# A four-layer graph network on one core: products of the identity in TensorE's waits

## The chip, the cores and the metric

The kernel runs on one core of a Trainium2 chip. The metric is the time on the device, in microseconds (us). A core has five engines that work side by side and wait for each other by semaphores: TensorE (PE; PEld is its loading of weights), VectorE (DVE), ScalarE (ACT), GpSimd (POOL), and SyncE (SP), which here issues the loads of the large matrix. TensorE's clock can be granted in full or in part, and the profile records which.

## What is computed

x is 4096 x 64, adj is 4096 x 4096 and sparse, with values of 0.05 to 1 where it is not zero. Four layers follow each other, each with `h = relu(layernorm(x))` and `x = x + layer(h, adj)`:

```
layer 0:  relu((adj @ h) @ W.T + b)
layer 1:  att = adj * sigmoid((2 + 2 * qm @ k.T) / att_scale + att_bias)
          support = att @ lorentz(h);   support / sqrt(|inner(support)|)
layer 2:  agg_i = sum_j adj_ij / deg_i * logmap(h_i, h_j);   expmap0(agg @ W + b)
layer 3:  mask = adj != 0;  w = mask * 0.5 ** (rank from the row's end, 100 neighbours at most)
          w @ (h @ W) + b
```

Layer 1's q and k are two more linear maps of the layer's own h, each scaled row by row. Layer 2 needs a square, a clamp, two logarithms and two exponentials for every pair (i, j). Layer 3 needs a running count of neighbours along each row.

## The kernel before, in words

adj is read transposed, in pieces of 128 x 1024 f32 (512 KB, "groups"): a group holds two chunks of 128 source rows for one block of 512 target rows. There are 8 blocks (`ib`) of 16 groups (`g`). Each layer reads the groups that it needs from memory again, through `feed` (SP's queue) into ten buffers, six of them kept for all layers. A buffer is free again when its last reader on each engine is done.

- Layer 0: `l0_sums` multiplies each group with the rows of h (`HA`), two matmuls of 64 columns side by side, into one bank `acc`; DVE adds the groups up for the degrees (`dg`). `before0` makes h from x, block by block, and group g needs the rows of block g/2. At the end of a block `after0` updates x, and `before1` makes q, k and the rows for layer 1.
- Layer 1: `l1_atts` (PE, into `mm`), `l1_sigmoids` (ACT), `l1_weights` (DVE, times adj), `l1_sums` (PE, into `acc`), in pairs of groups; at a block's end `after1` and `before2`.
- Layer 2: distances on PE (`l2_dists`), square on ACT, clamp on POOL, then ACT and DVE in turn, transposes on PE (`l2_turns`, into the banks `tr`), and two kinds of sums. It uses that a pair's distance is symmetric: blocks get shorter from one to the next.
- Layer 3: masks on DVE, counts and ranks in bf16 matmuls, powers of two on ACT (`wt`), sums in bf16.

Two banks `tr` serve everything that is small: transposes, small products and the degrees. `bank` takes one from the list `spare`, and `emptied` puts it back as soon as the reader of its content has been written into the program, which can be before that reader has run.

The order on each engine is fixed while the program is built. Each stage is a generator that yields the engine that its next step uses and the time from which it may run. `in_turn` always takes the step that can start first, by a clock kept in the source (`Pace`): `pace.free[engine]` is when an engine gets free, `pace.now` when the chosen step starts. `Pace.issue` moves an engine's clock on by the instruction's modelled cost, from the time when the engine and the tiles with known ready times are free. Tiles named in `KEPT` (x, HA, qT and others) have no such time, so PE's clock may lag behind the step's own start. Everything is issued through `InOrder.__getattr__` (line 129 in the profile), so the profile's groups are told apart by their tiles, not by lines. Each engine runs its instructions in that order.

Of the kernel before, what the change touches and what calls it, by code (L numbers as in the profile page):

```python
# [18 lines left out]
P = 128  # L19
# [6 lines left out]
G = 2  # L26
NG = NC // G
LEFT = (3, 7, 11, 15)
EARLY = 12
BEHIND = NG - CB // G  # L30
LATE = BEHIND - CB // G
# [105 lines left out]
def kernel(ctx: ExitStack, tc: tile.TileContext, a: dict, out: bass.AP):  # L137
# [4 lines left out]
    pace = Pace()  # L142
    PE, DVE, ACT, POOL = (
        InOrder(tc, e, pace, name)
        for e, name in (
            (nc.tensor, "PE"), (nc.vector, "DVE"), (nc.scalar, "ACT"), (nc.gpsimd, "POOL"),
        )
    )
# [11 lines left out]
    x = keep.tile([P, NC, D], F32, name="x")  # L160
# [4 lines left out]
    ident = const.tile([P, P], F32, name="ident")  # L165
# [168 lines left out]
    spare = [0, 1]  # L334

    def bank():
        k = spare.pop(0)
        t = ps_tr.tile([P, W], F32, tag=f"tr{k}", name="tr", bufs=1)
        in_use.append((t, k))
        return t  # L340

    def emptied(t):
        k = [k for k in in_use if k[0] is t][0]
        in_use.remove(k)
        spare.append(k[1])
# [334 lines left out]
    tail = []  # L680
# [7 lines left out]
    def advance(entry):  # L688
        pace.latest = 0.0
        old = entry.pop("bank", None)  # L690
        before = len(in_use)
        if not entry["evicts"]:
            if entry["slot"] is None:
                entry["slot"] = 1 - tail[0]["slot"] if entry is not tail[0] else (
                    1 - tail[1]["slot"] if len(tail) > 1 and tail[1]["slot"] is not None else 0
                )
            slot["now"] = entry["slot"]
        entry["evicts"] = False
        on = next(entry["gen"], tail)
        if on is tail:  # L700
            tail.remove(entry)
        else:
            entry["on"], entry["at"], entry["need"] = on, pace.latest, None
            if isinstance(on, tuple):
                entry["on"], entry["need"] = on
        if len(in_use) > before:
            entry["bank"] = in_use[-1][0]
        if old is not None:
            emptied(old)
# [4 lines left out]
    def in_turn(threads):  # L714

        waiting = [[gen, next(gen, None)] for gen in threads]
        waiting = [t for t in waiting if t[1]]
        while waiting or tail:  # L720
            best = None
            for k, entry in enumerate(tail):
                if k < 2 or entry["evicts"]:
                    need = entry["need"]() if entry["need"] else 0.0
                    if need is None or (entry["on"] == TURN and not spare):
                        continue
                    start = max(entry["at"], pace.free[entry["on"]], need)
                    if "tables" in opened and "weighed" not in work[FIRST]:
                        start += 2 * EPS
                    if best is None or start < best[0]:  # L730
                        best = start, entry
            for thread in waiting:
                on, need = thread[1]
                t = need()
                if t is not None and (best is None or max(t, pace.free[on]) < best[0] - EPS):
                    best = max(t, pace.free[on]), thread
            pace.now, what = best
            if what in tail:
                advance(what)
                continue  # L740
            pace.latest = 0.0
            what[1] = next(what[0], None)
            if what[1] is None:
                waiting.remove(what)


    st = {
# [4 lines left out]
    opened = {}  # L752
# [67 lines left out]
    def group(layer, ib, g):  # L820
        degree = (g in LEFT and 0 < ib < NB - 1) == (layer == 1)
        return {"layer": layer, "ib": ib, "g": g, "degree": degree, "left": 1 + degree, "at": 0.0}
# [6 lines left out]
    l1 += [group(1, ib, g) for ib in range(2, NB) for g in range(NG)]  # L829
    order = l0[: len(l0) - EARLY] + [d for pair in zip(l0[len(l0) - EARLY :], l1) for d in pair]  # L830
    order += l1[EARLY:]
    done = {}
# [571 lines left out]
    def l3_sum():  # L1404
# [25 lines left out]
    last = work[L3_AT:]  # L1430
    order23 = work[:L3_AT] + [d for pair in zip(last, l3) for d in pair] + l3[len(last) :]
    in_turn([
        feed(order, "early"), feed(order23, "second"), second_tables(), second_part(), third_part(), l2_loads2(),
        l0_sums(), l1_sums(), l1_weights(), l1_sigmoids(), l1_atts(),
# [59 lines left out]
```

## Time and profile before

| | |
|---|---|
| time, median of 3 runs | 1186.83 us (1185.45 to 1261.08) |
| profiled execution | 1186.61 us, its span 1184.6 us |
| mean granted TensorE clock | 0.976 |
| busy: PE, DVE, ACT, POOL | 1078.5, 929.3, 783.1, 324.3 us |
| matmul records on PE | 5367 |
| read from memory | 269.68 MB, 229 GB/s over the span |
| adj groups loaded | 512 |

The page's rows of digits show the span in 40 slices, PEclk the granted clock in tenths. In a row of the timeline the first number is the start in us from the span's start, the second the time until the last of the merged instructions ended, then engine, operation, out<-in tiles, shapes and count; square brackets hold the engine's idle time ahead of it and what ended that. Ends of matmuls are modelled, and a 512-column f32 matmul takes two records. By the timeline, layer 0 lasts until about 220 us (mixed with the start of layer 1), layer 1 until 486, layer 2 until about 957, and layer 3 until the end.

### The profile page before, as it was taken

The page shows a single profiled execution, that of the slowest core. Times are in us where ns is not written, and L with a number is a line of the kernel's source. Part 1 is how long each engine was busy: PE and PEld are TensorE (multiplying, and loading weights), DVE is VectorE, ACT ScalarE, POOL GpSimd, SP SyncE. Part 2 cuts the span into 40 slices and gives each one's busy share as a digit, 9 for nine tenths or more (in the row PEclk, how much of TensorE's full clock was granted, in tenths as well). Part 3 has the DMA queues.
Part 4 walks back from the last instruction along what each step waited for, and adds up shares of the span by engine and source line. Part 5 has one row for each costly group of instructions (what it writes and reads, how often), then busy time and mean ns, then how long its engine had stood idle before and what let it go on. Part 6 is the DMA issues. An engine that isn't in the chain of part 4 may idle for free.

```text
span 1184.6 us, 15638 instructions
## 1 busy us (share of the span) xinstructions
PE 1078.5 (91%) x5367; PEld 449.7 (38%) x5392; DVE 929.3 (78%) x1523; ACT 783.1 (66%) x1250; POOL 324.3 (27%) x172
## 2 busy tenths in 40 slices
PE   3899999999999999889989989999889789999997
PEld 1234444333333333244444444444344333333332
DVE  6888888869988988688888888898989985555550
ACT  1055456777767766789988778787876655555554
POOL 2222321102000010344454464464654420000000
PEclk9898999999999999899999999999998999999999
DMA  7899999865777765535434534444364389888830
GB/s 275 330 405 350 401 378 348 303 216 199 245 249 235 249 232 192 195 107 196 162 128 172 175 121 166 160 150 163 113 206 151 124 343 367 321 314 312 303 112 9
DMA packets 77191, 271.76 MB, mean 229 GB/s; under 512 B 10040, under 2 KB 11064, under 8 KB 77112
## 3 DMA queue, kind: packets, MB, share of 16 engines
q1 hardware_dynamic: 75456, 270.57, 63.7%
q8 instruction: 42, 0.69, 0.2%
q10 hardware_dynamic: 1656, 0.20, 0.1%
q14 instruction: 37, 0.30, 0.1%
HBM read 269.68 MB, written 1.05 MB: 229 GB/s over the span
## 4 chain that ended last, share of the span: by engine, by line
PE 49%; DVE 18%; ACT 11%; issue 10%; POOL 8%; DMA 3%; SPq 0%; ACTq 0%; POOLq 0%; DVEq 0%
PE acc L129 23%; PE mm L129 17%; PE tr L129 8%; DVE dg L129 5%; POOL v L129 4%; ACT wt L129 3%; DVE w L129 3%; ACT v L129 2%; DMA adj<-in_adjT_dram 2%; ACT t L129 2%; DVE t L129 2%; POOL lo_s L129 1%; DVE sig L129 1%; ACT sig L129 1%; POOL ln_r L129 1%
## 5 line engine op out<-in xcount | busy, mean ns | idle before, releaser
L129 PE MATMUL acc<-w,HA 128*65 128x256 f32 (+1 forms) x736 | 256.3, 485 | 13.0 <-DVE others L129 7.1
L129 POOL TENSOR_SCALAR v<-v 128x1024 f32<-128x1024 f32 x72 | 204.8, 2845 | 211.5 <-ACT v L129 205.4
L129 ACT ACTIVATE wt<-mm 128x1024 uint16<-128x1024 f32 x124 | 120.3, 1021 | 94.1 <-PE mm L129 94.1
L129 ACT ACTIVATE sig<-mm,att_b,att_a 128x1024 f32<-128x1024 f32 x128 | 148.3, 1202 | 40.9 <-PE mm L129 39.9
L129 DVE TENSOR_TENSOR sig<-sig,adj 128x1024 f32<-128x1024 f32 x128 | 152.5, 1221 | 25.2 <-ACT sig L129 25.0
L129 PE MATMUL acc<-adj,HA 128*64 128x512 f32 x512 | 128.4, 639 | 24.3 <-DVE HA L129 24.1
L129 DVE TENSOR_TENSOR dg<-dg,adj 128x1024 f32<-128x1024 f32 x114 | 139.2, 1221 | 2.2 <-DMA adj<-in_adjT_dram 0.6
L129 PEld LDWEIGHTS acc<-w,HA 128*65 128x65 f32 x736 | 98.1, 143 | 104.7 <-issue 56.6
L129 PE MATMUL mm<-qT,kT 64*128 64x512 f32 x512 | 129.5, 619 | 3.3 <-ACT sig L129 3.3
L129 PE MATMUL acc<-sig,HL 128*64 128x512 f32 x512 | 123.3, 604 | 1.6 <-DVE sig L129 1.5
L129 DVE SCALAR_TENSOR_TENSOR t<-mm,t 128x1024 f32<-128x1024 f32 x72 | 83.6, 1161 | 44.4 <-ACT t L129 43.9
L129 PE MATMUL acc<-wt,S 128*64 128x512 bf16 (+1 forms) x479 | 97.7, 387 | 3.5 <-issue 2.4
L129 PE MATMUL mm<-RT,LT 64*128 64x512 f32 (+1 forms) x288 | 79.7, 631 | 15.9 <-DVE t L129 15.2
L129 ACT ACTIVATE t<-t 128x1024 f32<-128x1024 f32 x72 | 72.6, 1008 | 31.9 <-DVE t L129 31.3
L129 ACT ACTIVATE v<-mm 128x1024 f32<-128x1024 f32 x72 | 69.8, 970 | 30.7 <-PE mm L129 30.6
L129 POOL TENSOR_TENSOR ln_r<-ln_v,minus_half 128x4 f32<-128x4 f32 x32 | 49.3, 1542 | 148.7 <-DVE ln_v L129 148.7
L129 DVE TENSOR_TENSOR w<-t,adj 128x1024 f32<-128x1024 f32 x72 | 84.0, 1167 | 1.5
L129 DVE SCALAR_TENSOR_TENSOR t<-t,v 128x1024 f32<-128x1024 f32 x72 | 83.7, 1163 | 1.8 <-ACT t L129 0.9
L129 ACT ACTIVATE v<-v,minus 128x1024 f32<-128x1024 f32 x72 | 78.4, 1089 | 7.8 <-POOL v L129 7.7
L129 DVE TENSOR_TENSOR w<-tr,adj 128x512 f32<-128x512 f32 x120 | 77.5, 681 | 1.1 <-PE tr L129 1.1
L129 PE MATMUL tr<-ident,t 128*128 128x128 f32 x480 | 66.1, 280 | 11.9 <-DVE t L129 8.2
L129 DVE TENSOR_SCALAR RT<-adj 128x1024 bf16<-128x1024 f32 x74 | 50.4, 698 | 33.3 <-PE mm L129 33.0
(208 smaller groups left out, 1395.6 us busy)
## 6 DMA issues: line engine op xcount, KB each, us to landing
adj<-in_adjT_dram SPq DMA_DIRECT2D x512, 512.0 KB, 4.8
x<-in_x_dram SPq DMA_DIRECT2D x4, 256.0 KB, 3.7
out_dram<-h SPq DMA_DIRECT2D x8, 128.0 KB, 2.8
b<-in_b_dram ACTq DMA_DIRECT2D x2, 32.0 KB
W<-in_W_dram ACTq DMA_DIRECT2D x3, 16.0 KB, 4.4
W0T<-in_W0T_dram ACTq DMA_DIRECT2D x2, 16.0 KB, 3.4
W1T<-in_W1T_dram ACTq DMA_DIRECT2D x1, 16.0 KB, 3.4
W1T<-in_b_dram ACTq DMA_DIRECT2D x1, 0.2 KB
```

The lines of the kernel that those rows point to most:

```text
L129: done = self.tc.keep_in_program_order(getattr(self.engine, op)(*args, **kw))
```

## The change

Each time that `in_turn` has chosen a step on PE, a new function `keep_warm` looks at how long, by the source's clock, PE will have waited for it. If that is 0.6 us or more, a bank `tr` is spare and layer 3 has not been opened, it takes a bank and issues f32 products of the 128 x 128 identity with itself (at the very first place, with 128 columns of x), as many as fit in the wait less 0.2 us at 0.28 us each, 24 at most. Nothing reads them. The bank is given back at once.

```
+WAIT = 0.6
...
             pace.now, what = best
+            on = what["on"] if what in tail else what[1][0]
+            if on == "PE":
+                keep_warm(pace.now - pace.free["PE"])
             if what in tail:
...
+    def keep_warm(wait):
+        if wait < WAIT or not spare or "third" in opened:
+            return
+        t = bank()
+        cold = not pace.shape
+        for _ in range(min(int((wait - 0.2) / 0.28), 24)):
+            PE.matmul(
+                t[:, 0:P], ident, x[:, 0:2, :].rearrange("p c d -> p (c d)") if cold else ident,
+                start=True, stop=True,
+            )
+        emptied(t)
```

The products are issued through the same layer as everything else, so they move PE's clock in the source, and with it the choice of later steps. They use PE and a bank; no other engine and no queue gets an instruction more.

## The prediction

> **What bounds the kernel now.** I read the page first (busy shares, the clock row, the chain), then cut the span where the granted clock changes, then the timeline of TensorE around each place where the change puts instructions.
>
> ```profile
> PE 1078.5 (91%) x5367; PEld 449.7 (38%) x5392; DVE 929.3 (78%) x1523; ACT 783.1 (66%) x1250; POOL 324.3 (27%) x172
> PEclk9898999999999999899999999999998999999999
> PE 49%; DVE 18%; ACT 11%; issue 10%; POOL 8%; DMA 3%; SPq 0%; ACTq 0%; POOLq 0%; DVEq 0%
> ```
>
> TensorE is busy 91% of the span and holds half of the chain that ended last. Its clock is near full nearly everywhere: the mean is 0.976. Even if every cold moment sat on the path, little could be won. Cutting at the clock's steps shows where they are:
>
> ```profile
> 31.20:38.00 6.80, 5.90 (x14) 1.67 (x16) 6.20 (x16) 0.93 (x3) 3.17 (x3) 0.51 0.86 301
> 92.60:99.50 6.90, 6.90 (x23) 3.32 (x24) 6.73 (x12) 4.45 (x22) 1.91 (x1) 0.51 0.90 338
> 99.50:488.60 389.10, 376.45 (x1798) 145.76 (x1794) 325.27 (x594) 258.86 (x583) 58.25 (x34) 1.00 0.77 272
> 488.60:498.80 10.20, 8.44 (x20) 2.63 (x20) 8.67 (x16) 7.22 (x11) 5.62 (x3) 0.51 0.57 213
> 611.50:614.90 3.40, 2.93 (x10) 1.44 (x7) 3.33 (x6) 3.37 (x5) 1.97 (x2) 0.51 0.00 0
> 946.00:952.80 6.80, 6.58 (x21) 3.31 (x21) 5.90 (x12) 3.43 (x6) 2.37 (x1) 0.51 0.34 99
> ```
>
> The columns after the bounds are the length, the busy time of PE, PEld, DVE, ACT and POOL, then the granted clock and the DMA share. There are eleven such half-clock stretches, each about 3.4 us or a multiple of it (41.4, 505.7, 700.2, 775.3, 840.2 and 891.4 are the others). Together they last 58 us, so 29 us is the ceiling of the gain. (16.7 to 21.0 is cold too: there is no record of it, but loads of weights come 0.62 us apart, and 0.29 later.) Layer 1 (99.5 to 488.6) has none. Layers differ in their limit: layer 0 from 60 to 210 us has a DMA share of 0.9 to 1.0; layer 1 has PE busy 233.6 of 240 us; in layer 2 PE, DVE, ACT and POOL take turns in the chain.
>
> **What the Trainium skill says.** "TensorE: Matmul & The Clock Gate", section "What's actually happening": the default clock is half, a free-running window of 3413 ns is watched, and a busy one gives the full clock. The trace agrees: 0.5 and 1.0 only, and stretches that are multiples of 3.41 us. The same page, "HAM oscillation — how this bites in real kernels", gives the rule that only idle gaps over about 3.4 us let the clock fall. The trace disagrees: before the stretch at 611.5 the longest idle time of PE is 1.72 us. A window less than about half busy is enough (1.7 us of 3.4 there; 1.4 of 3.4 before 31.2). Its section "What overlaps and what doesn't" has matmuls in strict order: so a filler that stands before a needed matmul and isn't done delays it. The prices below come from the trace.
>
> **The price of one product.** The added product is f32, 128 columns out, as the one with WqkT (65 rows instead of 128):
>
> ```profile
> 92.71 2.02 PE L129 MATMUL tr<-WqkT,columns 65*128 65x128 f32 x8
> 94.66 1.98 PE L129 MATMUL acc<-adj,HA 128*64 128x512 f32 x4
> ...
> 203.01 1.16 PE L129 MATMUL tr<-WqkT,columns 65*128 65x128 f32 x8
> 204.10 0.65 PE L129 MATMUL acc<-adj,HA 128*64 128x512 f32 x2
> ```
>
> Each f32 product is two records, so these are four products: 1.09 us to the next start at full clock, 0.27 each (0.224 start to start inside the batch), and 1.95/4 = 0.49 at half clock (0.43 start to start). I take 0.224 and 0.43 for long batches.
>
> **The change, part by part.** The built programs differ by 199 added products: 24 ahead of the first sum of layer 0, 61 among its first 14 groups, 39 in layer 1, 25 where layer 2 starts, 41 in its later blocks, 9 ahead of layer 3. That is 45 us of PE work at 0.224. Nothing is removed. Because products advance the source's clock for PE, the order in layers 0 and 1 also shifts a little (the first after0 comes three groups earlier, transposes trade places with sums); from the end of layer 1 on the orders agree. No load moves on SP's queue.
>
> *Start of layer 0.*
>
> ```profile
> 16.70 7.53 PE L129 MATMUL acc<-adj,HA 128*64 128x512 f32 x24 [16.70 <-DVE HA L129]
> 24.52 1.94 PE L129 MATMUL acc<-adj,HA 128*64 128x512 f32 x8 [0.30 <-DVE HA L129]
> ...
> 42.16 10.18 PE L129 MATMUL acc<-adj,HA 128*64 128x512 f32 x40 [3.42 <-DVE HA L129]
> ```
>
> The first 24 wait for the first quarter of x (4.4 us) and end by 4.4 + 24 x 0.43 = 14.7 even cold: free, ahead of 16.7. Then comes the odd piece: 24 products stand between the first group and the second, which is ready at the same time. From 16.7 to 42 PE has 14 groups (0.43 us warm) and 48 products: 6 + 10.8 = 16.8 us. With the clock cold until 21.0, as now, add 2 to 4 us: done by about 37; 13 products more, 2.9 us, about 40. The last HA rows come at 41.7 in any case, because of DVE's constants. Group 14 is then no later. Behind the products wait the releases of buffers: SP issues loads 10, 11, 12 now at 18.7, 21.2, 22.7; load 11 would go at about 25 and 12 at 28. Loads 14 to 21 go from 28.6 to 36.9 anyway, DVE's additions need load 11 first at 35.6. So 0, with bounds -1 and +10.
>
> *Layer 1.* No cold stretch, so nothing to win, and PE is the limit. Where products go, the real waits are shorter than those of the source's clock:
>
> ```profile
> 249.22 2.23 PE L129 MATMUL mm<-qT,kT 64*128 64x512 f32 x8 [0.68 <-ACT sig L129]
> ...
> 357.77 2.23 PE L129 MATMUL mm<-qT,kT 64*128 64x512 f32 x8 [0.21 <-ACT sig L129]
> ...
> 390.61 1.99 PE L129 MATMUL mm<-qT,kT 64*128 64x512 f32 x8
> ```
>
> At 249.2 nine products (2.0) face 0.68 idle and 0.16 of drain: +1.2. At 357.8 three (0.67) face 0.37: +0.3, and again at 427.6. At 390.6 and 460.3 three face no wait: +0.6 each. Four single ones: +0.2 each. Four at 285.8 are taken up by the 1.54 us wait at 288.4, five pairs just fit into waits near 0.5. Sum +3.8; the waits at 252, 259 and 284 give back about 1.5: +2.2, bounds +0.5 and +5 (order included).
>
> *Start of layer 2.* The chain runs through cold PE work:
>
> ```profile
> 492.78 1.12 PE L129 MATMUL tr<-ident,t 128*128 128x128 f32 x4
> ...
> 494.09 3.65 PE L129 MATMUL acc<-w,HA 128*65 128x512 f32 x4 [0.19 <-PE tr L129]
> ```
>
> The same four records take 1.93 at 499.67. Nine products fill 487.3 to 489.4, within an idle 2.77, so the window before 488.6 is 2.7 of 3.4 busy: the clock should hold. The sum saves 1.7, the distances after it 0.6; six products and one more then stand in the way for about 0.3: -2.0, bounds -3.5 and +1.
>
> *Block ends of layer 2.* At 605.4 PE waits 1.31 and gets four products (0.9), free. The cold comes later, from the idle 1.72 before 610.32. There no bank is free and nothing is added. The three at 612.3 come in the cold: 1.3 us against 0.68 free, +0.6 on PE, but the chain runs over POOL's clamp at 614.79, not PE. -0.5 in all, bounds -3 and +2.
>
> *Start of layer 3.* 946 to 952.8 is cold and dense on PE (6.58 of 6.80), and in the chain. Five products fall into the idle 1.67 before 944.65: the window before 946 rises from 1.1 to 2.2 of 3.4 busy, over half. Warm, 6.8 us of work take 3.4; DVE is close behind, so -2.5, bounds -3.4 and 0.
>
> Sum: 0 + 2.2 - 2.0 - 0.5 - 2.5 = -2.8. The profiled execution took 1186.61 us with a span of 1184.6; less 2.8 is 1183.8. The median, 1186.83, is 0.2 above that execution: 1184.
>
> **The rivals.**
> 1. *Products in the way at the start: slower.* If the clock is cold through 16.7 to 42, 14 groups at 0.9 and 48 products at 0.49 take 36 us: group 14 starts about 53 plus 13 x 0.49, late by up to 17; loads wait on the releases, and the DMA-bound layer 0 can't make it up except for about 6 us in which SP waits for DVE (36.9 to 43.3). It decides from about 42 us on. 1184 + 11 = 1195. For: the second batch has no wait behind it. Against: dense work warmed the clock within 4.3 us at 16.7 to 21.0.
> 2. *The clock does not hold.* The windows run free, and most products stand where PE was warm. Then only layer 1 counts: 1187 + 2.5, about 1189. For: the block ends' gap stays empty.
> 3. *All of it helps.* The windows at the block ends and at 92.6 turn warm as well, and each half of 3.4 us counts: 1184 - 10 = 1174. Against: chain on POOL, layer 0 bound by DMA.
>
> **How the numbers follow.** Forecast (1178 to 1188) 0.5, rival 1 0.2 (1190 to 1200), rival 2 0.2 (1187 to 1191), rival 3 0.1 (1170 to 1178). The range leaves out half of rival 3 and the upper part of rival 1: 1176 to 1197. Over 2% is 23.7 us, about what a measurement here can tell from no change; 29 us is the ceiling of a gain, 17 the worst start: faster 0.02, same 0.93, slower 0.05.
>
> **What would show it.** Right: clock 1.0 from 488 to 499 and from 946 to 953; group 14 at 42 us and layer 0's end where they were; layer 1 some 2 us longer between its first distances and the table load; half clock still near the block ends. Wrong: the first sums spread past 42 us with DMA share below 0.9 after it (rival 1), or half clock at layer 2's and 3's start (rival 2). An order that lets ACT run dry in layer 1 would be outside of all of these.

## The result, and the profile after

The changed kernel takes 1184.57 us (median of 12 runs, 1181.51 to 1187.42). The kernel before took 1185.35 us beside it, so the ratio is 0.9992 with a 95% interval of 0.998 to 1.0004: 0.9 us less, between 2.4 less and 0.5 more. One run of before, 1261.08 us, was in a slow state and is left out of the ratio. All differences in us below that are not read from a trace are worked out from such ratios, and can differ by a few tenths from the differences of the medians. The profiled execution took 1184.66 us with a span of 1182.9.

The time is the one forecast, within 0.6 us. The median of before was 1.5 us lower in this comparison than in the first runs, so the gain is 0.9 us and not the 2.8 of the sum. The sum was also put together from wrong parts, as the stages show: that the time fits so closely is luck.

The page of the kernel after, with the lines that answer to those shown of before:

```profile
span 1182.9 us, 16429 instructions
PE 1114.5 (94%) x5765; PEld 494.6 (42%) x5790; DVE 929.3 (79%) x1523; ACT 783.8 (66%) x1250; POOL 321.1 (27%) x172
PEclk9999999999999999999999999999999889999999
PE 54%; DVE 17%; ACT 11%; issue 9%; POOL 6%; DMA 1%; SPq 0%; ACTq 0%; POOLq 0%; DVEq 0%
```

TensorE has 398 records more, two for each of the 199 products. It is busy 36 us longer, and its share of the chain rose from 49 to 54%, in a span that is 1.7 us shorter. The half clock fell from 58 to 24 us in these two profiles (the last, slack microseconds of the program left out). If every one of these moments had held up the end, about 17 us would have been won.

The stretches of the kernel after, cut where the prediction looked (columns as before: length; busy time of PE, PEld, DVE, ACT and POOL; granted clock; DMA share; GB/s):

```profile
21.00:42.00 21.00, 21.00 (x121) 11.06 (x120) 19.51 (x52) 1.76 (x5) 7.40 (x17) 1.00 0.65 244
60.00:203.80 143.80, 140.47 (x747) 62.19 (x743) 128.11 (x201) 81.34 (x306) 32.30 (x20) 1.00 0.99 390
203.80:482.30 278.50, 276.53 (x1302) 107.39 (x1300) 227.37 (x444) 195.81 (x356) 30.59 (x18) 1.00 0.69 229
482.30:499.00 16.70, 14.88 (x90) 8.79 (x88) 13.22 (x21) 14.49 (x20) 10.31 (x6) 1.00 0.53 192
938.50:941.90 3.40, 3.40 (x13) 2.24 (x12) 2.85 (x11) 0.68 (x2) 0.00 (x0) 0.50 0.02 5
942.80:953.00 10.20, 9.91 (x53) 4.61 (x52) 9.10 (x21) 5.74 (x9) 2.37 (x1) 1.00 0.44 157
955.50:958.90 3.40, 3.11 (x13) 0.54 (x12) 3.14 (x8) 1.76 (x4) 1.51 (x2) 0.50 0.90 325
```

The same cuts of layers 0 and 1 in the kernel before:

```profile
60.00:211.50 151.50, 143.86 (x750) 63.77 (x746) 130.34 (x202) 81.50 (x305) 38.00 (x21) 0.98 0.97 377
211.50:485.60 274.10, 267.62 (x1224) 97.71 (x1222) 227.54 (x447) 194.87 (x358) 29.41 (x19) 1.00 0.69 232
```

Three things are to be seen. Layer 0, after its start, is 7.7 us shorter at a DMA share of 0.99 instead of 0.97, where the sum had put nothing; 1.8 us of that is a first HA row (the rows of h that all of layer 0 waits for) that ended later in this profile of before. Layer 1 is 4.4 us longer, and TensorE is busy 8.9 us more in it. Around the start of layer 3 the clock is full from 942.8 to 953, as forecast, but half before it and again after it.

The table puts the stages of all the traces side by side, in us. "Layer 0" runs from the end of the first HA row to the end of the last sum (the row's own end differs by up to 1.9 us between executions, whatever the kernel); "layer 1" from there to its last sum; "start" from the third to the seventh distance of layer 2 (a distance is one group's `l2_dists`); "rest" from there to the end. "Cold" counts the half-clock stretches of 3.4 us in layer 1. "Order" is that of the work in layers 0 and 1; the kernels with old order or no products stem from the experiments below.

| kernel | layer 0 | layer 1 | cold | start | rest |
|---|---|---|---|---|---|
| before | 194.9 | 274.0 | 0 | 27.0 | 667.5 |
| before, again | 194.1 | 277.3 | 2 | 25.4 | 666.2 |
| after | 189.0 | 278.5 | 0 | 24.8 | 671.2 |
| after, again | 189.0 | 280.1 | 1 | 26.0 | 671.6 |
| new order, no products | 189.5 | 280.3 | 2 | 25.8 | 666.8 |
| new order, none in layer 0 | 190.2 | 278.5 | 0 | 25.6 | 669.2 |
| new order, none in layer 1 | 189.0 | 278.7 | 1 | 24.8 | 671.2 |
| old order, all products | 195.8 | 279.6 | 0 | 24.8 | 671.9 |
| new order in layer 0 alone | 189.3 | 276.7 | 1 | 26.7 | 667.3 |
| new order in layer 1 alone | 193.3 | 281.9 | 2 | 25.4 | 667.4 |
| old order, later blocks' products | 194.5 | 277.3 | 2 | 25.4 | 669.8 |
| old order, layer 3's products | 194.9 | 277.3 | 2 | 27.7 | 671.0 |
| old order, products at layer 2's start | 192.8 | 274.0 | 0 | 24.8 | 666.0 |
| new order in layer 0, products at layer 2's start | 190.7 | 276.7 | 1 | 24.8 | 666.2 |

A half-clock stretch in layer 1 costs 1.65 us: 277.3 less 274.0 is two of them, 280.1 less 278.5 one, and the other kernels with layer 1's old order and no products there fit (274.0 with none, 277.3 twice with two). The kernel before has none in one execution and two in another. That its first trace has no cold stretch there is therefore chance. A trace is one execution: those of layer 3's products (1192.34 us) and of layer 2's start (1179.11) are the slowest and the fastest of 22 of their kernels, so only stages are compared here, and gains are taken from the ratios.

### The profile page after: what moved, and what is told of

Same layout as the page of the kernel before. It is cut to its first block, busy times and chain, and to the rows that moved or that the text cites. A ratio compares the mean times of both kernels' runs of the same rounds, so it can differ in the third digit from the quotient of the medians.

```text
span 1182.9 us, 16429 instructions
## 1 busy us (share of the span) xinstructions
PE 1114.5 (94%) x5765; PEld 494.6 (42%) x5790; DVE 929.3 (79%) x1523; ACT 783.8 (66%) x1250; POOL 321.1 (27%) x172
## 4 chain that ended last, share of the span: by engine, by line
PE 54%; DVE 17%; ACT 11%; issue 9%; POOL 6%; DMA 1%; SPq 0%; ACTq 0%; POOLq 0%; DVEq 0%
PE acc L130 26%; PE mm L130 18%; PE tr L130 10%; DVE dg L130 4%; ACT wt L130 3%; POOL v L130 3%; ACT v L130 2%; DVE w L130 2%; ACT t L130 2%; DVE t L130 2%; DVE sig L130 1%; DMA adj<-in_adjT_dram 1%; POOL r_nn L130 1%; ACT sig L130 1%; POOL lo_s L130 1%
## 5 line engine op out<-in xcount | busy, mean ns | idle before, releaser
L130 PE MATMUL acc<-w,HA 128*65 128x256 f32 (+1 forms) x736 | 250.7, 477 | 10.3 <-DVE w L130 5.2
L130 ACT ACTIVATE sig<-mm,att_b,att_a 128x1024 f32<-128x1024 f32 x128 | 148.9, 1201 | 53.1 <-PE mm L130 52.5
L130 PE MATMUL acc<-adj,HA 128*64 128x512 f32 x512 | 120.8, 601 | 2.1 <-DVE HA L130 2.1
L130 ACT ACTIVATE v<-v 128x1024 f32<-128x1024 f32 x72 | 72.8, 1012 | 2.3
```

What stands on the lines that cost most here:

```text
L130: done = self.tc.keep_in_program_order(getattr(self.engine, op)(*args, **kw))
```

## The experiments

The theory after the result: products advance the source's clock for TensorE, which lags behind the steps otherwise, so the change is two changes: another order of the work in layers 0 and 1, and products. The rival is the prediction's account, in which only the products count.

**The order alone.** The source's clock is moved as by the products, and the bank is rotated, but no product is issued.

```
+        moving = x[:, 0:2, :].rearrange("p c d -> p (c d)") if cold else ident
+        n = min(int((wait - 0.2) / 0.28), 24)
+        if not issued(pace.now):
+            spare.append(spare.pop(0))
+            for _ in range(n):
+                pace.issue("PE", "matmul", (Unwritten, ident, moving), dict(start=True, stop=True))
+            return
```

`issued` returns False here; `Unwritten` stands for the bank in the source's clock.

> The order of the change without its 199 products: the source's clock is moved as if they were issued. Theory P (the products keep the clock up, and the order is of no account): layer 0's last sum ends near 211 us as before, half-clock stretches as before (about 58 us), total 1185. Theory O (the order of layers 0 and 1 is what moves layer 0): its last sum ends near 204 as with the change, layer 1 takes some 4 us less than with the change since nothing stands in its way, and the total is 1179 to 1183.

1183.09 us beside 1186.32, ratio 0.9975 [0.9966, 0.9983], so 3.0 us faster, and layer 0 is 189.5 against 194.9 and 194.1. The order alone gains 3.0 us where the whole change gained 0.9. Layer 1 does not come out 4 us shorter than with the change, as theory O had it: it takes 280.3 us, of which two cold stretches are 3.3.

**The products alone.** The order of before, and the 199 products ahead of the same steps (two batches of layer 1 are one pair of groups later), issued past the source's clock.

```
+PRODUCTS = {
+    0: 24, 2: 24, 4: 9, 8: 3, 12: 3, 16: 3, 20: 3, 24: 3, 28: 13, 582: 9,
...
+    2204: 4, 2220: 3, 2300: 1, 2356: 4, 2372: 3, 2517: 3, 2521: 1, 2525: 5,
+}
...
+            if on == "PE" and pace.steps in PRODUCTS and spare:
+                products(PRODUCTS.pop(pace.steps), not pace.steps)
```

> The order of the kernel before, with the 199 products ahead of the same steps as in the change. Theory P: layer 0's last sum ends near 204 us, half-clock time about 28 us, layer 2's start 2 us shorter, layer 1 4 to 5 us longer, total 1183 to 1186. Theory O: layer 0 ends at 211, layer 1 is 4 to 5 us longer, layer 2's start 2 us shorter, total 1187 to 1190.

1193.1 us, ratio 1.0053 [1.0033, 1.0073]: 6.3 us slower. That is more than theory O had (1187 to 1190). Layer 1 takes 279.6 us against 274.0, with no cold stretch in either; the rest takes 671.9 against 667.5 and 666.2. Products without their order lose, about as much in the rest as in layer 1.

**Without layer 1's products, and without layer 0's.** The order is that of the change; the products of one layer move the source's clock only.

```
 def issued(now):
-    return False
+    return not 60.0 < now < 495.0
```

and

```
-    return False
+    return now > 60.0
```

> The order of the change, with the 39 products of layer 1 left out. If these products are what makes layer 1 longer: from the end of layer 0 to the last sum of layer 1 takes 274 us as before instead of 278.5, total 4 us below the change, about 1180.5. If layer 1's new order is what costs: no difference to the change, 1184.5.

> The order of the change, with the 85 products of layer 0's first 41 us left out. Theory P: layer 0's last sum ends near 211 us, half-clock stretches there as before, total 1191. Theory O: its last sum ends near 204 or earlier, total 1184 or less.

Without layer 1's products: 1186.22 us, 1.0005 [0.9991, 1.002]. Without layer 0's: 1185.09, 0.999 [0.9976, 1.0004]. Against the change (0.9992) that is 1.5 us slower without layer 1's products and 0.2 faster without layer 0's, each known to about 2 us, so neither differs measurably from the change. The first run's total is nearer to the second of its forecasts (1184.5) than to the first (1180.5), and its layer 1 takes 278.7 us and not 274: most of what makes it longer is the order. What layer 1's products do there is seen in TensorE's waits for the results of `l1_sigmoids`, ahead of the next `l1_atts`. The line gives the wait in all, the number of times and the longest, for the kernel before:

```profile
PE mm L129 <- ACT sig L129: 3.3, 8, 0.7
```

for the new order with no product:

```profile
PE mm L141 <- ACT sig L141: 7.9, 13, 2.3
```

and for the change:

```profile
PE mm L130 <- ACT sig L130: 0.7, 3, 0.3
```

The new order makes `l1_atts` wait for ScalarE's sigmoids, 4.6 us more, and the products then lie in that wait. ScalarE in its turn waits longer for TensorE, 52.5 us instead of 37.6; before and new order:

```profile
ACT sig L129 <- PE mm L129: 37.6, 36, 3.2
```

```profile
ACT sig L141 <- PE mm L141: 52.5, 42, 3.9
```

The products are not free for all that: with the cold stretches taken off, layer 1 takes 277.0 us in the new order without its products (278.7 less one, 280.3 less two) and 278.5 with them. The time of the whole kernel does not show this 1.5 us.

**The order of one layer.** No products; the source's clock is moved only up to 60 us of its own time (the new order in layer 0, the old one nearly throughout layer 1), or only from 60 to 495 us (the old order in layer 0, the new one in layer 1).

```
-        if wait < WAIT or not spare or "third" in opened:
+        if wait < WAIT or not spare or pace.now > 60.0:
```

and

```
+        if wait < WAIT or not spare or not 60.0 < pace.now < 495.0:
```

> No products; the source's clock is moved as if they were issued, but only in the first 60 us. That gives layer 0 the order that the change has, and layer 1 the order of before from its 20th group or so on. Theory: the new order of layer 0 gains and the new order of layer 1 loses. Then layer 0's last sum ends 3 to 7 us earlier than before, layer 1 takes 274 us from there (280 with the whole order of the change), total 1179 to 1182. If layer 0's gain in the trace was luck of the clock's windows: total 1185 to 1186.5. If the two orders are coupled, a layer 0 that ends earlier only makes layer 1 wait: layer 1 takes 278 to 280 us again.

> The order that the products bring to layer 1, without any product, and with the order of before in layer 0: the source's clock is moved only between 60 and 495 us of its own time. Theory from the traces: that order makes TensorE wait for ScalarE's sigmoids (7.9 us instead of 3.3) and costs about 3 us in layer 1: 1189, with the time from the end of layer 0 to the last sum of layer 1 near 277 us against 274. Rival from the medians (the new order throughout 1183.1, in layer 0 alone 1182.6): it costs half a microsecond, and the rest of those 3 us was half-clock stretches in those executions: 1186.7.

In layer 0 alone: 1182.62 us beside 1186.21, 0.9967 [0.9956, 0.9978], 3.9 us faster. In layer 1 alone: 1189.15 beside 1186.08, 1.0022 [1.0013, 1.0031], 2.6 us slower, and its 281.9 us less two cold stretches (3.3) are 278.6 against 274.0. One order gains, the other loses. Two stages missed their forecasts: this layer 1 was to take 277 us, and that of the first kernel 274, where it took 276.7 with one cold stretch, so about 1 us of layer 0's gain is lost again in layer 1. The waits in this last kernel are those of the new order:

```profile
PE mm L141 <- ACT sig L141: 8.8, 15, 2.3
```

**The products of one place.** The order of before, with the 25 products where layer 2 starts, the 41 in its later blocks, or the nine ahead of layer 3.

```
+PRODUCTS = {1158: 9, 1164: 6, 1168: 1, 1176: 2, 1178: 4, 1184: 3}
```

```
+PRODUCTS = {1286: 2, 1508: 4, 1524: 3, 1724: 1, 1780: 4, 1796: 3, 1956: 1, 2012: 4,
+            2028: 3, 2148: 1, 2204: 4, 2220: 3, 2300: 1, 2356: 4, 2372: 3}
```

```
+PRODUCTS = {2517: 3, 2521: 1, 2525: 5}
```

> The kernel before with the 25 products at layer 2's start alone. Theory: they keep the clock at full from 488 to 499 us, so layer 2's fifth distance comes 2 to 3 us earlier counted from layer 1's last sum, and the total falls by 1.5 to 2.5 us. If DVE's work on the first blocks takes the time anyway: no change of the total (within 0.7 us).

> The kernel before, with only the 41 products that the change adds in the later blocks of layer 2, ahead of the same steps; the order of everything else is that of before. The prediction priced them at -0.5 us (bounds -3 and +2): 1185.7 beside 1186.2 for before. Theory that they stand in the way there (the traces with them take about 4 us more from the seventh distance of layer 2 to the end): 1188 to 1190, and the time from that distance to the last sum of layer 2 near 440 us instead of 436.6. Rival: that was the luck of where the clock's windows fell in those executions: 1186 +- 1, with that stage between 436 and 440 and fewer or more half-clock stretches to match.

> The kernel before, with only the nine products that the change adds ahead of layer 3. The prediction priced them at -2.5 us (bounds -3.4 and 0), because the clock would hold through the dense 6.8 us: 1183.7 beside 1186.2 for before, with full clock where layer 3 starts. Theory that the window before it is still under half busy, or falls elsewhere: 1186 +- 1 and half clock there. Theory that they stand in the way: above 1187.

Start of layer 2: 1184.63 us, 0.9987 [0.9974, 0.9999], 1.5 us faster, and 24.8 us in that stage, against 27.0 and 25.4. Later blocks: 1185.91, 0.9999 [0.9986, 1.0012], no difference that can be measured. Ahead of layer 3: 1187.1, 1.0014 [1.0004, 1.0024], 1.7 us slower where the prediction had 2.5 faster. The theory that the later blocks' products stand in the way (1188 to 1190) failed, that of layer 3's (above 1187) held.

The traces say why the last two don't gain. In the later blocks all distances, counted from the seventh, stand as in the kernel before to within 0.01 us up to the first place where products come. TensorE's timeline there, before (the second profile of it):

```profile
537.38 1.88 PE L129 MATMUL acc<-w,HA 128*65 128x512 f32 x4
539.19 1.13 PE L129 MATMUL mm<-RT,LT 64*128 64x512 f32 x4
```

and with the later blocks' products:

```profile
537.00 1.88 PE L132 MATMUL acc<-w,HA 128*65 128x512 f32 x4
539.32 0.71 PE L760 MATMUL tr<-ident 128*128 128x128 f32 x4 [0.44 <-DVE w L132]
539.96 1.13 PE L132 MATMUL mm<-RT,LT 64*128 64x512 f32 x4
```

The distances had no wait. Two products are put ahead of them, into a bank `tr` that DVE is still reading: TensorE waits 0.44 us for DVE, then multiplies for 0.64, and the next distance comes 1.14 us late (2.96 us after the sums' start instead of 1.81). From there to the last block the difference stays between 0.8 and 1.3 us, apart from single distances that are late for one block: the three and four products of each later block end cost nothing, and bring 0.2 us in all. The last block adds 1.5 us, in a half-clock stretch at 930.6. Five of the six traces with these products have a stretch at that place, about 12 us ahead of the end of the wait shown next, and none of the eight without; why is not shown. The ratio of this kernel shows no loss; its profiled execution took 2.6 us more than its median.

Ahead of layer 3, before (second profile):

```profile
940.36 0.43 PE L129 MATMUL tr<-ident,e 65*128 65x65 f32 x4 [1.59 <-DVE w L129]
940.86 3.38 PE L129 MATMUL acc<-w,HA 128*65 128x256 f32 x8
944.48 0.66 PE L129 MATMUL tr<-ident,l 128*64 128x128 f32 x4 [0.23 <-DVE l L129]
...
958.73 2.46 PE L129 MATMUL acc<-wt,S 128*64 128x512 bf16 x7
```

and with the nine products:

```profile
943.41 0.91 PE L759 MATMUL tr<-ident 128*128 128x128 f32 x6 [1.59 <-DVE w L131]
944.37 0.70 PE L131 MATMUL tr<-ident,e 65*128 65x65 f32 x4
944.86 0.74 PE L759 MATMUL tr<-ident 128*128 128x128 f32 x2
945.39 3.07 PE L131 MATMUL acc<-w,HA 128*65 128x256 f32 x8
948.30 1.28 PE L759 MATMUL tr<-ident 128*128 128x128 f32 x10
949.63 0.63 PE L131 MATMUL tr<-ident,l 128*64 128x128 f32 x4
...
963.79 3.78 PE L131 MATMUL acc<-wt,S 128*64 128x512 bf16 x16
```

The 1.59 us of waiting are still there, and the products come after them: they wait for the same DVE instruction as the work that they were to shorten the wait for. Counted from the end of that wait, the first products cost 0.96 us, the next 0.52, the sums are 0.71 shorter at a partly better clock, and the last five cost 1.33: together 2.1, so `tr<-ident,l` starts 6.22 us after the wait instead of 4.12. That is no luck of one execution: it is 4.1 in all eight traces without these products, 6.0 to 6.3 in five of the six with them, and 4.7 in the sixth, whose clock is full there.

The first sum of layer 3 comes 20.38 us after the wait. In this second profile of before it is 18.37, and in the first, with its half clock from 946.1 to 952.8, 20.13. The other six traces without these products fall into the same two kinds: 18.2 to 18.6 in three, 20.0 to 20.1 in three with 6.8 to 10.2 us of half clock there. With them it is 20.2 to 20.4 in five, 18.9 in the sixth. So the products do take away that half clock, and cost as much as it did. After the first sum layer 3 takes 223.9 to 225.0 us in the eight traces, and 225.3 to 226.5 in the six: all six have one more half-clock stretch 11 to 12 us after it, which none of the eight has.

**The kernel before once more, and the change once more.** No edit, one profile each.

> The kernel before once more, for its trace: if the clock's windows run free, the half-clock stretches lie elsewhere by up to 3.4 us and some come or go; if layer 0 has no half-clock stretch near 92 us, its last sum ends 2 to 3 us earlier than in the first trace, which would be luck and no gain of the change.

> The changed kernel once more, for where the clock's windows fall. Theory that the later products cost time whatever the windows do: from the seventh distance of layer 2 to the end again near 671 us. Rival, luck of the windows: another set of half-clock stretches and a time nearer to the 666.7 us of the kernels without those products.

Before: 1185.34 us, its span 1183.3. Its half-clock stretches lie elsewhere than in the first profile: two in layer 1, and two at 941.2 and 958.3 instead of the one from 946.1 to 952.8. The rest takes 666.2 us instead of 667.5. After: 1188.04 us, with one stretch in layer 1 and one at 512.1, and 671.6 us for the rest. That agrees with the theory that the later products cost time wherever the windows fall. How much of the 4 to 5 us (671.2 to 671.9 against 666.2 to 667.5) is clock can be read in part from the table: both executions of the change, and the kernels with all products and without layer 1's, have half clock in the same four places around layer 3's start, while the execution without layer 0's products, which has the same later ones, has only the last of the four (969.4). Its rest is 669.2. So about 2 us go with those three stretches, and 3.0 remain beside 666.2: 1.3 up to the last distance, 0.5 before the first sum of layer 3, and 1.2 after it, where the fourth stretch lies.

**What the runs point to.** The new order in layer 0 alone, and the 25 products where layer 2 starts: the two parts that gained.

```
+            if on == "PE":
+                keep_warm(pace.now - pace.free["PE"])
+                if pace.steps in PRODUCTS and spare:
+                    products(PRODUCTS.pop(pace.steps))
```

with `keep_warm` as in the order of layer 0 alone.

> Both of the two: the early order of layer 0 without products there, and the 25 products at layer 2's start. If the two gains are independent they add: 2 us below the early order alone, 1177 to 1180. If layer 2's start waits for something else than PE: the same as the early order alone.

1180.6 us, ratio 0.9954 [0.9942, 0.9967], so 5.5 us faster than before; the two parts alone add up to 5.4. It is the fastest kernel here, just above the 1177 to 1180 expected.

## Why the prediction was right or wrong

The time and the verdict were right: 1184.57 against 1184.0, no difference beyond 2%. The sum behind it was right by luck: a gain that it left out (layer 0's order) cancels a gain that did not come (layer 3's start), and before measured 1.5 us less than the time that it started from. Its steps:

- **Start of layer 0, 0: right as a sum, not in its step.** The prediction had group 14 no later. Products and sums run from 15.9 to 43.3 without a gap, group 14 starts at 43.3 instead of 42.2, and loads 11 to 13 go at 22.6, 28.6 and 29.1 instead of 21.3, 22.7 and 25.0. Counted from the first HA row and held against the first profile of before, group 14 is 2.9 us late, group 24 1.6, and group 48 is 0.3 early: the delay is made up. Leaving those products out changes nothing that can be measured. Rival 1 fell, and so did rival 3: half clock stays at three block ends of layer 2 (607.4, 771.2 and 887.3).
- **Order in layer 0: the step that failed first.** The prediction saw that "the order in layers 0 and 1 also shifts a little", and gave it no price in layer 0; that layer 0's end would stay where it was did not come. It is the largest term: -3.9 us [-5.2, -2.6] by the ratio, 4 to 5 by most of the traces (the new orders 189.0 to 190.7 us, the old without layer 0's products 192.8 to 194.9). The trace says where: the DMA share of 60 us onward rises from 0.97 to 0.99, and the issue of loads waits less for layer 1's and the block ends' work on DVE. The waits of SP's queue from 44 us to layer 0's end, before and after:

```profile
SPq L776 <- DVE sig L129: 9.7, 6, 4.3
SPq L776 <- DVE ln_m L129: 3.4, 1, 3.4
SPq L776 <- DVE h L129: 3.3, 3, 1.9
SPq L776 <- DVE ln_v L129: 1.8, 1, 1.8
```

```profile
SPq L794 <- DVE sig L130: 4.0, 5, 1.9
SPq L794 <- DVE h L130: 1.4, 2, 0.7
SPq L794 <- DVE ln_v L130: 1.2, 1, 1.2
```

  That is 18.2 us against 6.6; the waits for layer 0's own readers (`dg` and `acc`) grow by 3.2. They go with layer 0's order: the wait for `sig` is 4.0 in the new order without products, and 9.7 where layer 0 has the old order and layer 1 the new one. That they are the cause of the gain was not tested apart from the order.
- **Layer 1, +2.2 (bounds +0.5 and +5): sign right, mechanism wrong.** It measured +4.5 in the trace (278.5 against 274.0), within the bounds; against the second profile of before, with its two cold stretches, it is +1.2. The prediction had products standing in the way, in the old order. There they cost more than its upper bound: 5.6 us. In the new order it is largely the other case that it named as "outside of all of these": ScalarE runs dry (37.6 to 52.5 us of waiting) and TensorE waits for ScalarE in turn, +2.6 us by the ratio of that order alone. The products then fill TensorE's waits, and cost 1.5 us in the traces and nothing measurable in the time. "No cold stretch, so nothing to win" was read from one execution.
- **Start of layer 2, -2.0: right.** The clock is full from 482.3 to 499, the stage is 0.7 to 2.2 us shorter, depending on which profile of before it is held against, and those products alone bring -1.5 [-3.1, -0.1] by the ratio.
- **Block ends of layer 2, -0.5: right as a size.** The ratio gives -0.1 [-1.7, 1.4]. The products at the block ends are free, as worked out. A pair at 539, of which the prediction said nothing, costs 1.14 us.
- **Start of layer 3, -2.5: the other step that failed.** It measured +1.7 [0.5, 2.8]. The clock from 942.8 to 953 did become full, so the reading of the clock held there. Two things were missed. The products need a bank, and the bank that the first of them get is still to be read by DVE, so they run after the wait. And the 1.67 us before `tr<-ident,l` that five products were to fill is 0.23 in the other profile of before: it was wide only where the sums ahead of it ran at full clock. So the products stood in the way for up to 2.1 us, about what the full clock saves (20.13 less 18.37), and the half clock moved to other moments around that stage instead of going.

The rival in which the clock does not hold had its places wrong, but its conclusion, that little of 29 us can be had, is what the measured times say: products where they help bring 1.5 us.

What stays open: the ratios of the parts (order -3.0, layer 2's start -1.5, later blocks -0.1, layer 3's start +1.7, and for layer 1's products -1.5 as the difference of two ratios) add up to -4.4, and the change measured -0.9. Each has an interval of 1 to 2 us either way, and parts were measured in one order and not in the other. The traces say where most of the 3.5 us between them lies: with all the later products the rest takes 671.0 us in the mean of five traces, without any of them 666.8 in the mean of seven. That is 4.2 us, where the two parts by themselves give 1.6. Why they cost more together than apart was not tested.

## What to carry to other kernels

Filler work that goes through the scheduler's own bookkeeping changes the schedule too: run the new order without the filler, and the filler in the old order, before crediting either. Filler fits into a wait only if everything it needs, its output bank above all, is free before that wait ends; a bank that the program counts as free may still have a reader to run, and then the filler comes after the wait and delays what was waiting. A gain read from half-clock stretches in one profile is no more certain than their places: profile the kernel before twice first. And ask of every stretch whether its end holds up the program's end.

## What the runs showed of the hardware

- The same program had half-clock stretches in layer 1 in one execution (381.4 and 453.1 us) and none in another, with TensorE busy 267.6 of 274.1 us. Each cost 1.65 us of its 3.4.
- The prediction's rule, that a window less than about half busy is enough, can be counted. All 14 traces were cut into windows of 3.41 us in step with their own half-clock stretches. Of the windows at full clock, all 46 with TensorE busy less than 1.36 us were followed by half clock, 63 of the 174 between 1.36 and 2.05, and 14 of the 4338 above. Each of these 14 holds a whole batch of a block end, eight records of 64 columns (`tr<-twice,e` or `tr<-W0T,e`) and eight of one column (`tr<-ones_f,dg`); 100 other windows with such a batch stayed at full clock. So the share of busy time in the profile is not quite what the clock goes by; what it goes by there is not shown. The window ahead of the stretch at 381.4 in the second profile of before, and that stretch:

```profile
378.00:381.40 3.40, 3.08 (x24) 2.30 (x22) 2.42 (x3) 2.05 (x5) 0.00 (x0) 1.00 0.74 236
381.40:384.80 3.40, 3.40 (x8) 0.89 (x8) 1.83 (x8) 1.86 (x4) 1.01 (x1) 0.50 0.50 161
```

- The matmuls are in strict order, as the Trainium skill says in "TensorE: Matmul & The Clock Gate", section "The mechanism" of its part 3, under "What overlaps and what doesn't". The order is kept across a wait: at 539.3 a product that waits 0.44 us for its bank holds up distances that wait for nothing.
- Keeping TensorE busy removes half-clock stretches, and yet the time hardly moved. The two profiles of before have 58 and 38 us of them, the two of the change 24 and 31. 34 us less could be worth 17, and 0.9 came out.
